# Attention strips by three transfers a unit, and second-half maxima joined with the first keys' maxima by one instruction

## The chip, the core and the metric

The kernel runs on one NeuronCore of a Trainium2 chip. The metric is the device time of one execution in microseconds. A core has five engines that take their own instructions in order: TensorE (PE in the profile; PEld is its weight loads), VectorE (DVE), ScalarE (ACT), GpSimd (POOL) and SyncE (SP), which here only issues transfers (DMAs). An engine waits for another by semaphores. Matrix products go into PSUM, which is used here in banks of 128 x 512 float32.

## What is computed

Four blocks follow each other on x of shape (4, 1024, 256), each added to its input after a layer norm: an attention with 16 heads, a gated recurrence (FFN), a delta-rule attention, and the FFN again. The change touches the first block only:

```python
c_kv = x @ W_dkv.T
q = (x @ W_dq.T @ W_uq.T).reshape(B, T, nh, hs)          # 16 heads of 16
q_lat = einsum('bqhd,hdl->bhql', q, k_eff)               # k_eff from W_dq, W_uq, W_uk
attn = einsum('bhql,bkl->bhqk', q_lat, c_kv) / sqrt(hs)
attn = softmax(where(causal, attn, -inf), axis=-1)
y = einsum('bhql,hld->bqhd', einsum('bhqk,bkl->bhql', attn, c_kv), v_eff)
```

The kernel brings the latent form down to 16 rows a head for queries and keys, and folds the two value projections into one matrix, `ve`.

## The kernel before

**Units and passes.** The attention works in 16 units: 4 batches times 4 groups of 4 heads. A unit's scores are computed twice. As "first" (`ps_s1`, queries in PSUM's partitions) they yield the maximum of each row; as "second" (`ps_s2`, keys in the partitions) they yield exp(score - maximum), the weights. `quad(i, s)` does step s of ten (`STEPS`, L54) for the second pass of unit i and the first pass of unit i + 1 side by side, so that stage i works on two units; stage -1 has only the first pass of unit 0. A step is a piece of keys times queries, 384 or 512 columns wide, for four heads. Each head has its own group of 32 rows of the PE array, so four matmuls with 32 rows run at once.

**Strips.** To hold float32 accuracy with products of rounded numbers, keys and queries are split into a high part and a remainder. A head's 32 rows of `q` hold 16 rows of high parts and 16 rows of remainders; `kh` (keys' high parts) and `kl` (their remainders) hold their 16 rows twice. The high and low parts of all heads stand in DRAM in `kall` and `qall`; `feature` (L272) computes 128 rows by 512 columns of them (PE, ACT cast, DVE subtraction) and SP writes them (L287). `heads(i, j)` (L313) fetches head j's strips of unit i by six transfers of 16 rows by 4 KB (L324), so 24 a unit, all on SP's queue. Three buffers each of `kh`, `kl` and `q` rotate over the units. Unit 0's strips are made without DRAM by `first_feature` (L296), with `wk0` and `wq0`, whose columns are in the strips' order, and `second_half` (L124), which is 1 in the rows of remainders.

**Maxima.** `finish` (L416) reduces a first-pass bank on DVE. Where a piece has masked keys, L424 adds the mask and takes the maximum, starting from a constant for queries 0 to 511, and from `m0` for queries 512 to 1023; `m0` is the maximum over keys 0 to 511, taken by L430 in steps 3 to 6. Each L424 is followed by a read of the accumulator. `greatest(i, half)` (L464) turns a half's maxima: a PE transpose (L468), an ACT cast (L470), a DVE subtraction (L471), a write to DRAM `md` (L473) and two reads into `gr` (L475), which the second pass subtracts by a matmul with `minus`. Half 0 of unit i + 1 is called after step 4 of stage i; half 1 of unit i after step 0 of stage i, when the DVE operations of that step, of unit i + 1, have been issued.

**Order of the work.** The order is written out by hand (L519 to L606). All engines receive their instructions in the order in which the Python calls are made. `places[s]` lists what follows step s: features, projections, norms, `heads` and `greatest`. In stage -1 the remaining features of batch 0, `heads(1, 0..3)`, the values and `load(2)` are spread over steps 3 to 9 (L569), with the `heads` after all eight features. `values` runs two steps behind, between the two halves of a step. After stage 1, `load_ffn` (L567) issues 13 transfers on SP. PSUM has seven banks for scores and small products, taken in turn (`pss`, L74).

Of the kernel before, what the change touches and what calls it, by code (L numbers as in the profile page):

```python
# [10 lines left out]
F32 = mybir.dt.float32  # L11
# [3 lines left out]
ALU = mybir.AluOpType  # L15
AX = mybir.AxisListType
PSUM = bass.MemoryType.PSUM

P = 128
B, T, C = 4, 1024, 256  # L20
# [7 lines left out]
NH, HS = 16, 16  # L28
# [10 lines left out]
def attention(k, w, x):  # L39
# [6 lines left out]
    nc, tc = k.nc, k.tc  # L46
    NT = T // P
# [20 lines left out]
    with ExitStack() as es:  # L68
# [52 lines left out]
        qq = [wp.tile([P, T], F32R, name=f"q{i}") for i in range(3)]  # L121
        gr = [wp.tile([P, T], F32R, name=f"gr{i}") for i in range(2)]
        minus = wp.tile([P, P], F32R, name="minus")
        second_half = wp.tile([P, 1], F32, name="second_half")  # L124
        wk0, wq0 = (wp.tile([P, P], F32, name=n) for n in ("wk0", "wq0"))

        def first_rows():
            nc.gpsimd.memset(minus.bitcast(F32), -1.0)
            nc.gpsimd.memset(mb, 0.0)
            nc.gpsimd.memset(second_half, 1.0)  # L130
            nc.gpsimd.affine_select(
                out=mb, in_=mb, compare_op=ALU.is_ge, fill=NEG, base=0, pattern=[[1, P]], channel_multiplier=-1,
            )
            for j in range(4):
                d = second_half[ds(32 * j, 32), :]
                nc.gpsimd.affine_select(
                    out=d, in_=d, compare_op=ALU.is_ge, fill=0.0, base=-HS, pattern=[[0, 1]],
                    channel_multiplier=1,
                )
            for g in gr:  # L140
                nc.vector.memset(g.bitcast(F32), 0.0)

        VS = HS + 1
        vb = [wp.tile([P, NT, NH * VS + 32 - VS], F32, name=f"vb{i}") for i in range(2)]
# [26 lines left out]
        nc.scalar.activation(wq, ps.rearrange("p k m -> p (k m)"), AF.Copy, scale=1.0 / math.sqrt(HS))  # L171
        for a in range(2):
            nc.scalar.activation(
                wq0.rearrange("p (j a r) -> p j a r", j=4, a=2)[:, :, a],
                ps[:, 0, 0:64].rearrange("p (j r) -> p j r", j=4), AF.Copy, scale=-1.0 / math.sqrt(HS),
            )
        ps = pss.tile([P, KVL], F32, tag="s", name="ps_p1")
# [4 lines left out]
        nc.tensor.matmul(ps, p1, wdq, start=True, stop=True)  # L182
        for a in range(2):
            nc.scalar.copy(
                wk0.rearrange("p (j a r) -> p j a r", j=4, a=2)[:, :, a],
                ps[:, 0:64].rearrange("p (j r) -> p j r", j=4),
            )
        nc.scalar.copy(wk, ps)
# [83 lines left out]
        def feature(b, mc, n, name, wt, src, aside=False):  # L272

            bt = batches[b]
            if mc == n == 0:
                setattr(bt, name, dr.tile([2, C, T], F32R, tag=name, name=name))
            ps = pss.tile([P, 512], F32, tag="s", name="ps_f")
            nc.tensor.matmul(
                ps, wt[:, ds(mc * P, P)], getattr(bt, src)[:, ds(n * 512, 512)], start=True, stop=True
            )  # L280
            if aside:
                hl = sm.tile([P, 4, 512], F32, tag="p", name="hp", bufs=3)[:, 0:2].bitcast(F32R)
            else:
                hl = sm.tile([P, 2, 512], F32R, tag="hl", name="hl", bufs=2)
            nc.scalar.copy(hl[:, 0], ps)
            nc.vector.tensor_tensor(hl[:, 1], ps, hl[:, 0].bitcast(F32), ALU.subtract)
            nc.sync.dma_start(  # L287
                out=getattr(bt, name).bitcast(F32)[:, ds(mc * P, P), ds(n * 512, 512)].rearrange("a c t -> c a t"),
                in_=hl.bitcast(F32),
            )  # L290
# [5 lines left out]
        def first_feature(n, name):  # L296

            u, bt = units[0], batches[0]
            cols = ds(512 * n, 512)
            ps = pss.tile([P, 512], F32, tag="s", name="ps_f")  # L300
            keys = name == "k"
            nc.tensor.matmul(ps, wk0 if keys else wq0, (bt.ckv if keys else bt.qd)[:, cols], start=True, stop=True)
            if keys:
                nc.scalar.copy(u.kh[:, cols], ps)
                nc.vector.tensor_tensor(u.kl[:, cols], ps, u.kh[:, cols].bitcast(F32), ALU.subtract)
            else:
                hi = sm.tile([P, 2, 512], F32R, tag="hl", name="hl", bufs=2)[:, 0]
                nc.scalar.copy(hi, ps)
                nc.vector.scalar_tensor_tensor(
                    u.q[:, cols], hi.bitcast(F32), second_half, ps, ALU.mult, ALU.subtract  # L310
                )

        def heads(i, j):  # L313

            if j == 0:
                name_buffers(i)
            u = units[i]
            bt = batches[u.b]
            rs = ds(64 * u.g + HS * j, HS)
            k_, q_ = bt.kall.bitcast(F32), bt.qall.bitcast(F32)  # L320
            for a in range(2):
                to = ds(32 * j + HS * a, HS)
                for dst, src in ((u.kh, k_[0, rs]), (u.kl, k_[1, rs]), (u.q, q_[a, rs])):
                    nc.sync.dma_start(out=dst.bitcast(F32)[to, :], in_=src)  # L324

        def normed(b, after=False):

# [38 lines left out]
        def quad(i, s):  # L366
# [49 lines left out]
            def finish(one, j):  # L416
                ps = bank(one, j)
                if not one:
                    nc.scalar.activation(p[:, j, :width], ps[:, :width], AF.Exp)  # L419
                    return  # L420
                for at, qt, c0, n, _, _ in pieces:
                    if c0 + n == (qt + 1) * P:
                        junk = sm.tile([P, 512], BF16, tag="junk", name="junk")
                        nc.vector.tensor_tensor_reduce(  # L424
                            out=junk[:, :n], in0=ps[:, ds(at, n)], in1=mask[:, 512 - n :], scale=1.0,
                            scalar=-3e38 if qt < 4 else first.m0[:, j, qt - 4 : qt - 3],
                            op0=ALU.add, op1=ALU.max, accum_out=first.m[:, qt // 4, j, qt % 4 : qt % 4 + 1],
                        )
                    else:
                        nc.vector.tensor_reduce(  # L430
                            first.m0[:, j, qt - 4 : qt - 3], ps[:, ds(at, n)], AX.X, ALU.max
                        )
# [31 lines left out]
        def greatest(i, half):  # L464

            u = units[i]
            ps = pss.tile([16, P], F32, tag="s", name="ps_m")
            nc.tensor.transpose(ps, u.m[:, half].rearrange("p j q -> p (j q)"), k.ident)  # L468
            mT = sm.tile([16, 2, P], F32R, tag="mT", name="mT")
            nc.scalar.copy(mT[:, 0], ps)  # L470
            nc.vector.tensor_tensor(mT[:, 1], ps, mT[:, 0].bitcast(F32), ALU.subtract)  # L471
            d = dr.tile([16, 2, P], F32R, tag="md", name="md")
            nc.sync.dma_start(out=d.bitcast(F32), in_=mT.bitcast(F32))  # L473
            for a in range(2):
                nc.sync.dma_start(  # L475
                    out=u.gr.bitcast(F32)[ds(a, 4, step=32), ds(half * 512, 512)].rearrange("j (q t) -> j q t", q=4),
                    in_=d.bitcast(F32)[:, a].rearrange("(j q) t -> j q t", j=4),
                )
# [41 lines left out]
        with tc.manual_schedule():  # L520
# [19 lines left out]
            for f in rest[:2]:  # L540
                f()
            del rest[:2]
            for mc in range(KC):
                for n in range(2):
                    for name, wt, of in (("kall", wk, "ckv"), ("qall", wq, "qd")):
                        rest.append(
                            lambda mc=mc, n=n, name=name, wt=wt, of=of: feature(
                                0, mc, n, name, wt, of, name == "qall" or n == 1
                            )
                        )  # L550
            rest += [lambda j=j: vals(0, j) for j in range(0, NT, 2)]
            rest[-2:-2] = [lambda j=j: heads(1, j) for j in range(4)]
            rest.append(lambda: load(2))
            late = []
            LONG = (0, 1, 3, 4, 6, 7, 8, 9)
            for i in range(-1, NU):
# [8 lines left out]
                    late += [lambda g=g: first_cells(g) for g in "fic"]  # L565
                places = [[] for _ in range(NS)]
                if i < 0:  # L567
                    places[0] += rest[:2]
                    places[1] += rest[2:4]  # L569
                    for a, f in enumerate(rest[4:]):  # L570
                        places[3 + a * (NS - 3) // len(rest[4:])].append(f)
                    rest = []
                else:
                    for work, left in ((rest, NG - 1 - i % NG), (late, NG - i % NG)):
                        share = -(-len(work) // left) if left > 0 else len(work)
                        for a, f in enumerate(work[:share]):
                            places[LONG[a * len(LONG) // share]].append(f)
                        del work[:share]
                if i + 1 < NU:
                    places[4].append(lambda i=i: greatest(i + 1, 0))  # L580
                if 0 <= i < NU - 2:

                    for j in range(4):
                        places[2 + j].append(lambda i=i, j=j: heads(i + 2, j))
                if i >= 0:
                    units[i].p = {}
                    places[0].insert(0, lambda i=i: greatest(i, 1))
# [1055 lines left out]
```

## Time and profile before

| | us |
|---|---|
| median of 3 runs (lowest to highest) | 1326.14 (1324.3 to 1327.25) |
| the profiled execution | 1326.79 |
| its span, first to last instruction | 1325.1 |
| PE busy in the span | 1247.8 |
| DVE busy | 840.2 |
| ACT busy | 697.5 |
| POOL busy | 423.3 |

The mean granted clock of PE is 0.982. A line of the profile gives an operation with its line in the kernel, what it writes and reads, its partitions and sizes, how often it ran, its busy time and mean, and the idle time of its engine just before it with what ended that. In a timeline a line has the start, the length, and in brackets the idle time before it. SPq is SP issuing a transfer, not the transfer itself.

### The profile page before, as it was taken

The page shows a single profiled execution, that of the slowest core. Times are in us where ns is not written, and L with a number is a line of the kernel's source. Part 1 is how long each engine was busy: PE and PEld are TensorE (multiplying, and loading weights), DVE is VectorE, ACT ScalarE, POOL GpSimd, SP SyncE. Part 2 cuts the span into 40 slices and gives each one's busy share as a digit, 9 for nine tenths or more (in the row PEclk, how much of TensorE's full clock was granted, in tenths as well). Part 3 has the DMA queues.
Part 4 walks back from the last instruction along what each step waited for, and adds up shares of the span by engine and source line. Part 5 has one row for each costly group of instructions (what it writes and reads, how often), then busy time and mean ns, then how long its engine had stood idle before and what let it go on. Part 6 is the DMA issues. An engine that isn't in the chain of part 4 may idle for free. (4 is left out here: it accounts for less than half of the span.)

```text
span 1325.1 us, 36572 instructions
## 1 busy us (share of the span) xinstructions
PE 1247.8 (94%) x14596; PEld 776.4 (59%) x14596; DVE 840.2 (63%) x2440; ACT 697.5 (53%) x1626; POOL 423.3 (32%) x681
## 2 busy tenths in 40 slices
PE   7899899999999999999999999898988999899997
PEld 3454455545555555555444766665655677677886
DVE  6786678787787877886122454468879767533333
ACT  3266566666666666666623456445655544334432
POOL 1040002323033110122100245346888745535220
PEclk9799899999999999999999999999999999999999
DMA  3812621334221422220300223215364532333210
GB/s 96 208 51 70 186 67 48 79 96 146 68 53 41 133 79 59 67 51 4 112 17 0 78 75 90 80 26 166 99 169 112 139 90 75 111 102 85 64 64 32
DMA packets 118649, 112.23 MB, mean 85 GB/s; under 512 B 46672, under 2 KB 103504, under 8 KB 118480
## 3 DMA queue, kind: packets, MB, share of 16 engines
q1 hardware_dynamic: 95200, 100.39, 27.6%
q10 hardware_dynamic: 23280, 9.51, 2.7%
q8 instruction: 115, 1.88, 0.6%
q14 instruction: 54, 0.44, 0.1%
HBM read 65.22 MB, written 44.63 MB: 83 GB/s over the span
## 5 line engine op out<-in xcount | busy, mean ns | idle before, releaser
L419 ACT ACTIVATE p<-ps_s 128x512 f32<-128x512 f32 (+1 forms) x640 | 319.3, 554 | 199.7 <-PE ps_s L410 196.5
L410 PE MATMUL ps_s<-kh,q 32*128 32x512 f32 (+3 forms) x768 | 189.3, 425 | 8.8 <-DMA q<-qall 5.1
L430 DVE TENSOR_REDUCE m<-ps_s 128x1 f32<-128x512 f32 x256 | 163.0, 681 | 34.9 <-PE ps_s L410 34.5
L410 PE MATMUL ps_s<-q,kh 32*128 32x512 f32 (+3 forms) x768 | 163.2, 424 | 0.4
L488 PE MATMUL ps_y<-p,vb 128*32 128x512 f32 (+3 forms) x1536 | 158.3, 500 | 1.1 <-ACT ys L494 1.0
L410 PE MATMUL ps_s<-kl,q 32*128 32x512 f32 (+3 forms) x768 | 151.7, 357 | 0.0
L424 DVE CUSTOM_DVE_ANT_0 junk<-ps_s,mask,m 128x512 bf16<-128x512 f32 (+3 forms) x256 | 126.4, 545 | 38.3 <-PE ps_s L410 37.6
L424 DVE CUSTOM_DVE_ANT_0 junk<-ps_s,mask 128x512 bf16<-128x512 f32 (+3 forms) x256 | 112.3, 486 | 48.9 <-PE ps_s L410 48.5
L410 PE MATMUL ps_s<-q,kl 32*128 32x512 f32 (+3 forms) x768 | 131.2, 359 | 0.0
L410 PEld LDWEIGHTS ps_s<-q,kh 32*128 32x128 f32 x768 | 73.9, 184 | 77.1 <-issue 45.8
L512 POOL TENSOR_TENSOR xa<-xa,yt 128x256 f32<-128x256 f32 x32 | 23.4, 731 | 275.7 <-DVE yt L508 275.7
L410 PEld LDWEIGHTS ps_s<-kh,q 32*128 32x128 f32 x768 | 89.1, 185 | 28.1 <-ACT p L419 9.8
L410 PE MATMUL ps_s<-gr,minus 32*128 32x512 f32 (+3 forms) x768 | 98.2, 365 | 6.1 <-DMA gr<-md 4.9
L391 PEld LDWEIGHTS <-identb 128*128 128x128 bf16 x512 | 34.4, 98 | 88.2 <-issue 85.8
L410 PEld LDWEIGHTS ps_s<-kl,q 32*128 32x128 f32 x768 | 81.4, 188 | 0.0
L205 POOL TENSOR_SCALAR rs<-mv 128x2 f32<-128x2 f32 x24 | 5.5, 230 | 236.6 <-DVE mv L204 236.6
L410 PEld LDWEIGHTS ps_s<-gr,minus 32*128 32x128 f32 x768 | 67.6, 187 | 19.7 <-DMA gr<-md 5.3
L1120 DVE SCALAR_TENSOR_TENSOR gate<-gate 128x256 f32<-128x256 f32 (+1 forms) x56 | 29.4, 524 | 76.3 <-ACT gate L1099 76.1
L1080 PE MATMUL ps_gate<-xnT,ffn_wi 128*128 128x256 f32 (+1 forms) x224 | 66.0, 418 | 3.5 <-DVE hh L1193 3.3
L1198 POOL TENSOR_TENSOR x<-x,hh 128x256 f32<-128x256 f32 x56 | 44.0, 800 | 75.0 <-ACT hh L1197 54.2
L772 PE MATMUL ps_kqv<-wa,h 128*128 128x512 f32 x128 | 65.5, 634 | 2.4 <-ACT h L762 2.3
L410 PEld LDWEIGHTS ps_s<-q,kl 32*128 32x128 f32 x768 | 67.2, 186 | 0.0
(228 smaller groups left out, 2626.5 us busy)
## 6 DMA issues: line engine op xcount, KB each, us to landing
x<-x SPq DMA_DIRECT2D x30, 512.0 KB
kh<-kall SPq DMA_DIRECT2D x120, 64.0 KB
kl<-kall SPq DMA_DIRECT2D x120, 64.0 KB
q<-qall SPq DMA_DIRECT2D x120, 64.0 KB
kall<-hl SPq DMA_DIRECT2D x14, 512.0 KB
qall<-hl SPq DMA_DIRECT2D x12, 512.0 KB
kept<-gs ACTq DMA_DIRECT2D x32, 192.0 KB
gl<-kept SPq DMA_DIRECT2D x32, 192.0 KB
```

Of the source, the lines that this page charges most:

```text
L205: nc.gpsimd.tensor_scalar(rs, mv[:, :, 1], EPS, None, ALU.add)
L391: nc.tensor.matmul(ps[:, ds(at, P)], identb, mb, start=x == 0 and (False, j) not in begun, stop=True, skip_group_check=True,)
L410: nc.tensor.matmul(ps[:, ds(at, n)], a, m, start=x == 0 and (one, j) not in begun, stop=last, skip_group_check=True,)
L419: nc.scalar.activation(p[:, j, :width], ps[:, :width], AF.Exp)
L424: nc.vector.tensor_tensor_reduce(out=junk[:, :n], in0=ps[:, ds(at, n)], in1=mask[:, 512 - n :], scale=1.0, scalar=-3e38 if qt < 4 else fir ...
L430: nc.vector.tensor_reduce(first.m0[:, j, qt - 4 : qt - 3], ps[:, ds(at, n)], AX.X, ALU.max)
L488: nc.tensor.matmul(u.y[ds(32 * j, 32), q0:], vb[u.b % 2][:, kt, ds((4 * u.g + j) * VS, 32)], u.p[s][:, j, ds(at, n)], start=kt == 0, stop= ...
L512: nc.gpsimd.tensor_tensor(xs, xs, yt.rearrange("p n j d -> p n (j d)"), ALU.add)
L772: nc.tensor.matmul(dst, hT(c, kc), wt[:, kc, :], start=kc == 0, stop=kc == KC - 1)
L1080: nc.tensor.matmul(ps, f["w" + "fic"[j]][:, kc, ds(m * P, P)], k.xnT[:, kc, t, ds(at, width)], start=kc == 0, stop=t == 0 and kc == KC - 1,)
L1120: nc.vector.scalar_tensor_tensor(acts[1], acts[1], 1.0, acts[2], ALU.add, ALU.mult)
L1198: nc.gpsimd.tensor_tensor(x[:, b, :], x[:, b, :], h, ALU.add)
```

## The change

Strips: `heads` now issues one transfer of 128 rows for each of `kh`, `kl` and `q`, called for x = 0, 1, 2 after steps 2, 3 and 4. For keys, 64 rows of DRAM are read with each row repeated; for queries the high part and the remainder of a row follow each other. So a head's 32 rows now alternate between the two parts. `wk0`, `wq0` and the column vector (now `odd`, summed from the identity by one DVE reduction instead of a memset and four selects on POOL) follow that order.

Stage -1: the features of the first 128 rows are placed after steps 2 and 3, the three `heads` of unit 1 at the head of the work after step 4, the other features after steps 4 to 7, the values after steps 7 to 9. All eight features use tiles of the pool of `p` (six did before).

Maxima: L424 starts from the constant in both halves, and `greatest(i, 1)` first joins `u.m[:, 1]` with `u.m0` by one DVE maximum of 128 x 16.

```diff
-                nc.gpsimd.affine_select(
-                    out=d, in_=d, compare_op=ALU.is_ge, fill=0.0, base=-HS, pattern=[[0, 1]],
...
+            nc.vector.tensor_reduce(odd, k.ident[:, ds(1, P // 2, step=2)], AX.X, ALU.add)
...
-                wq0.rearrange("p (j a r) -> p j a r", j=4, a=2)[:, :, a],
+                wq0.rearrange("p (j r a) -> p j r a", j=4, a=2)[:, :, :, a],
...
-            rs = ds(64 * u.g + HS * j, HS)
-            k_, q_ = bt.kall.bitcast(F32), bt.qall.bitcast(F32)
-            for a in range(2):
-                to = ds(32 * j + HS * a, HS)
-                for dst, src in ((u.kh, k_[0, rs]), (u.kl, k_[1, rs]), (u.q, q_[a, rs])):
-                    nc.sync.dma_start(out=dst.bitcast(F32)[to, :], in_=src)
+            rs = ds(64 * u.g, 64)
+            if x < 2:
+                dst, src = (u.kh, u.kl)[x], bt.kall.bitcast(F32)[x, rs].unsqueeze(1).broadcast_to([64, 2, T])
+            else:
+                dst, src = u.q, bt.qall.bitcast(F32)[:, rs].rearrange("a r t -> r a t")
+            nc.sync.dma_start(out=dst.bitcast(F32), in_=src)
...
-                            scalar=-3e38 if qt < 4 else first.m0[:, j, qt - 4 : qt - 3],
+                            scalar=-3e38,
...
             u = units[i]
+            if half:
+                nc.vector.tensor_tensor(u.m[:, 1], u.m[:, 1], u.m0, ALU.max)
             ps = pss.tile([16, P], F32, tag="s", name="ps_m")
...
-                            lambda mc=mc, n=n, name=name, wt=wt, of=of: feature(
-                                0, mc, n, name, wt, of, name == "qall" or n == 1
-                            )
+                    for y, (name, wt, of) in enumerate((("kall", wk, "ckv"), ("qall", wq, "qd"))):
+                        first[2 + n if mc == 0 else 4 + 2 * n + y].append(
+                            lambda mc=mc, n=n, name=name, wt=wt, of=of: feature(0, mc, n, name, wt, of, True)
...
-            rest[-2:-2] = [lambda j=j: heads(1, j) for j in range(4)]
-            rest.append(lambda: load(2))
+            for y in range(3):
+                first[4].insert(y, lambda y=y: heads(1, y))
+            for j in range(0, NT, 2):
+                first[NS - 3 + (j + 2) // 4].append(lambda j=j: vals(0, j))
+            first[NS - 1].append(lambda: load(2))
...
-                    for j in range(4):
-                        places[2 + j].append(lambda i=i, j=j: heads(i + 2, j))
+                    for y in range(3):
+                        places[2 + y].append(lambda i=i, y=y: heads(i + 2, y))
```

## The prediction

> **What bounds the kernel now.** I read the page's busy shares, then the table by 10 us stretches, then what PE waited for, and last the timeline of three places. The page's slices first (each is 33 us; the attention is the first 19):
>
> ```profile
> PE   7899899999999999999999999898988999899997
> ...
> DVE  6786678787787877886122454468879767533333
> ...
> PEclk9799899999999999999999999999999999999999
> ```
>
> PE is nine tenths busy, except in slices 1, 2 and 5. After the attention PE runs matmuls back to back to 752 us, so what the attention gains or loses should arrive at the end one to one. The weak places in the stretches (columns: length, PE, PEld, DVE, ACT, POOL busy, granted clock, DMA share, GB/s):
>
> ```profile
> 50.00:60.00 10.00, 7.01 (x27) 3.77 (x25) 4.03 (x20) 1.67 (x3) 0.00 (x0) 0.50 1.07 122
> 60.00:70.00 10.00, 7.88 (x68) 4.47 (x66) 6.53 (x29) 3.83 (x9) 3.89 (x6) 0.50 0.57 135
> ...
> 150.00:160.00 10.00, 5.41 (x30) 1.97 (x34) 2.65 (x5) 2.54 (x5) 0.72 (x1) 0.66 0.52 154
> ```
>
> At 50 to 70 us, step 0 of unit 0, PE waits at half clock for the strips of unit 1; SP issues the last of 24 at 58.26:
>
> ```profile
> 58.26 0.30 SPq L324 DMA_DIRECT2D q<-qall  x1
> ```
>
> ```profile
> 56.27 0.76 PE L410 MATMUL ps_s<-kh,q 32*128 32x512 f32 x1 [2.54 <-DMA q<-qall]
> ...
> 62.29 0.76 PE L410 MATMUL ps_s<-kh,q 32*128 32x512 f32 x1 [2.12 <-DMA q<-qall]
> ```
>
> At 149.67 PE stands 4.91 us for gr, queued on SP behind load_ffn. Everywhere else in the attention PE is full by the page. That is only partly true: it waits for banks inside its overlapped matmuls, as the next part shows.
>
> **1. The join (the largest term).** L468 transposes the maxima of a unit's second half at the end of step 0 of the next stage. Before, these maxima are finished one step earlier. After, the join stands ahead of the transpose on DVE, and the order of instructions in the changed kernel puts it behind all four mask-and-max operations of step 0, which belong to the next unit. The transpose gains a wait on DVE. PE and DVE at this place in unit 3, before:
>
> ```profile
> 185.97 0.28 PE L468 MATMUL ps_m<-ident,m 128*16 128x128 f32 x1
> 186.08 0.27 PE L391 MATMUL ps_s<-mb,identb 128*128 128x128 bf16 x2
> 186.29 0.43 PE L410 MATMUL ps_s<-q,kh 32*128 32x384 f32 x1
> 186.71 0.44 PE L410 MATMUL ps_s<-kh,q 32*128 32x384 f32 x1
> ...
> 187.83 0.86 PE L488 MATMUL ps_y<-p,vb 128*32 128x256 f32 x16
> ```
>
> ```profile
> 186.71 0.69 DVE L424 CUSTOM_DVE_ANT_0 junk<-ps_s,mask 128x512 bf16<-128x512 f32 x1
> 187.32 0.08 DVE L424 DVE_READ_ACCUMULATOR2_ANT m<- 128x1 f32 x1
> 187.32 0.27 DVE L471 TENSOR_TENSOR mT<-ps_m,mT 16x128 fp32r<-16x128 f32 x1
> ```
>
> PE reaches L468 at 185.97; DVE is through with the four at 187.32, 1.35 us later. The join has no row: bounded below by the 0.08 us of a read of the accumulator, above by the 0.27 of the mT subtraction; I take 0.20, from the delta stage's m<-m,mt 128x30 (0.204). PE starts 0.06 after a DVE end (hl ends at 315.61, the gr matmul behind it starts at 315.67). So PE stands 1.35 + 0.20 + 0.06 = **1.6 us**. Queued behind L468 are all later matmuls: features, then step 1. The distance is 1.3 to 1.4 in all of units 1 to 14; unit 15 has no next unit and no wait.
>
> What is given back: step 1 in unit 3 already waits for banks. From its first strip product (186.29) to its values (187.83) are 1.54 us; in units where a latent projection stands between, and DVE and ACT catch up meanwhile, the same work takes 0.72. After a stall of 1.6 the banks are free, so 0.82 comes back. By this measure: units 3, 4, 7, 8, 12, 13, 14 lose 0.8 each (5.6); unit 11 (1.32 there) loses 1.0 and unit 6 (1.07) loses 1.3; units 1, 5, 9, 10 have nothing to give back, 1.6 each (6.4). Sum **+14.3 us**; bounds 10 (0.7 each) and 22.4 (1.6 each). Unit 2 loses nothing: its 4.91 us for gr simply become shorter. mT, md and gr run 1.2 to 1.6 later, but so does PE, and gr is used three steps on.
>
> Does a stall of 1.6 us lower the clock? The nearest row says no:
>
> ```profile
> 1130.13 1.13 PE L1080 MATMUL ps_gate<-xnT,ffn_wi 128*128 128x256 f32 x4 [1.60 <-DVE hh L1193]
> ```
>
> The stretch 1125 to 1135 around it has a granted clock of 1.00; the gap of 4.91 gave 0.66.
>
> **2. Strips in three transfers, unit 1's issued earlier.** 24 issues of 64 KB become 3 of 512 KB; bytes stay the same. Before, SP spaced the issues some 0.5 us; from the first (45.26) to the last (58.26) are 13.0 us. Large transfers moved 276 to 343 GB/s (load_ffn, 140 to 148 us), so 1.5 MB needs some 5 us. In the changed order the three stand behind only four of the features' writes, not eight. The first four writes come from steps 2 and 3; the fourth was issued at 37.70 before, so I expect about 36, its landing near 38.5, the strips by 44. They are wanted at 52, so the wait goes. What is late next: nothing but the clock, which fell at 46.4 while PE was merely sparse, and stays 0.50 there for all I can see. Step 0 of unit 0 lasted 52.09 to 63.58, 11.5 us. Step 1, at the same clock and without a wait, lasted 3.2 for 384 columns with 0.7 of masks; for 512 that is 2.5 x 1.33 + 0.7 = 4.0. With the new join wait 5.7. Gain 5.8, and DVE (9.93 of 10 us busy in 40 to 50) reaches unit 0 some 0.5 earlier through part 3: **-6 us**. Bounds: -11 if the clock is full there (step 0 then 3 us, steps 1 and 2 a us shorter each), and +1 if the strips still come late. The features' eight buffers now rotate through three tiles; the eighth cast waits for the fifth write, about 45 us, when it is due anyway: nothing, or 2 us at worst.
>
> [...] Here the stretch 40 to 50 shows PE 9.50 of 10 us busy and a clock of 0.82. [...]
>
> **3. Constant start of the second half's maxima.** Two rows, equal shapes, with and without the start from m0:
>
> ```profile
> L424 DVE CUSTOM_DVE_ANT_0 junk<-ps_s,mask,m 128x512 bf16<-128x512 f32 x60 | 42.6, 747 | 14.7 <-PE ps_s L410 14.3
> ...
> L424 DVE CUSTOM_DVE_ANT_0 junk<-ps_s,mask 128x512 bf16<-128x512 f32 x56 | 36.4, 687 | 9.3 <-PE ps_s L410 9.0 <-issue 0.2
> ```
>
> 60 ns x 16 a unit = 1 us of DVE, less 0.2 for the join. Most lies beside PE: DVE waits for PE before half of these. PE's and its weight loads' waits put down to L424 are 7.6 us in all, most of it before unit 0. I take **-1.5**; bounds 0 and -7.6.
>
> **4. Unit 2's gr.** md is issued at 148.70, paced by load_ffn from 139.6, which doesn't move. The gap shrinks from 4.9 to 3.3 (that is the unit's free join wait), and the half clock of 6.8 us may be shorter: **-1**; bounds 0 and -4.
>
> Costed at nothing: SP's freed issue time (idle otherwise); the order of rows (the strided casts of wk0 and wq0 run before x's features need them); four selects fewer on POOL and one reduction more on DVE (both ahead of the first load's landing); two features' buffers from another tile.
>
> **The sum**, on the profiled execution (span 1325.1, 1326.79 with what lies around it, 0.65 above the median 1326.14): 1326.79 + 14.3 - 6 - 1.5 - 1 = **1332.6 us**.
>
> **Rivals.**
> *The start outweighs the join.* Place: unit 0. If PE is at full clock there, part 2 gives -11; with part 3 at -4, part 4 at -2 and the join at its lower bound of 10, the sum is -7: 1320. It decides from the point where parts 2 and 3 together pass 14 us. For it: the half clock is this kernel's own doing at 43 to 46 us. Against: the same sparse work stays there.
> *Nothing is given back.* If step 1's bank waits come from the latency of exp and maximum rather than from being late, they stay: 22.4 - 6 - 1 = +15.4: 1342. If the clock also fell at each stall, several us more. For it: ACT also has mT to cast, behind the stall. Against: the 0.72 in three units.
> *The three transfers are not faster.* If a transfer with a repeated row runs on a part of the engines only, 1.5 MB could take the old 12 us or more, and unit 0 waits as before: part 2 is 0 and the sum +11.8: 1338.6. For it: no row shows such a transfer. Against: rows of 4 KB as before, 64 of them outermost.
> [...]
>
> **Chances.** Forecast 0.58 (1328 to 1338; 0.08 of it within 0.2%); start outweighs 0.20 (0.15 faster, 0.05 within); nothing given back 0.13; transfers not faster 0.09. 0.2%, 2.7 us, is about what a measurement of this kernel tells from no change. Faster 0.15, same 0.13, slower 0.72. Range 1321 to 1342: it takes in the bounds of the join and most of the start.
>
> **What would show it.** Right: L468 of every second transpose idle about 1.6 us and released by the join; no wait for q at 52 to 63; L424 all near 687 ns at 512; step 0 of unit 0 near 6 us; the attention's end some 6 us later. Wrong: no PE gap at L468, or gaps of 1.6 with units as long as before (then PE's slack was larger than I measure), or a clock of 1.00 through 50 to 60.

## The result and the profile after

The changed kernel takes 1340.09 us (median of 4 runs, 1337.64 to 1340.77) beside 1326.7 (4 runs, 1324.3 to 1329.36): a ratio of 1.0096, 95% interval 1.0078 to 1.0115. The forecast was 1332.6. Slower was right, but the loss, 13.4 us, is more than twice the 5.8 of my sum. The profiled execution took 1340.77 us, its span is 1338.8, the mean granted clock 0.978 (0.982 before). In the quoted lines of the changed kernel the line numbers are its own: maximum with mask L418, join L462, transpose L464, strips L318.

The page's slices after the change (33 us each):

```profile
PE   7899899999999999999999989999888999999997
...
DVE  6876677677777777777132444467978767534333
...
PEclk9799899999989999999999999989999999999999
```

DVE is down a tenth here and there, and the row of the clock has something new: an 8 in the twelfth slice (368 to 402 us), in the middle of the attention, where before stood only nines. The table by stretches, at the places shown before (columns as there):

```profile
50.00:60.00 10.00, 7.80 (x73) 4.61 (x71) 8.14 (x39) 5.23 (x11) 1.13 (x3) 0.95 0.76 248
60.00:70.00 10.00, 9.89 (x101) 5.71 (x100) 6.89 (x29) 4.92 (x11) 5.62 (x6) 0.71 0.29 107
150.00:160.00 10.00, 9.61 (x73) 3.58 (x69) 5.30 (x10) 6.51 (x13) 0.00 (x0) 0.77 0.58 202
```

**The start did what was forecast.** 50 to 60 us holds 73 matmuls where it held 27. The strips of unit 1 are three issues on SP, from 37.57 us on, and the DMA view of 30 to 60 us (40 slices of 0.75 us) shows 366, 388 and 333 GB/s from 39.75 to 42 us, where the bytes are all theirs. The 407 behind 44 us counts the next feature's write too. The strips are in by 46 us, six before they are wanted:

```profile
37.57 0.63 SPq L318 DMA_DIRECT2D kh<-kall  x1
38.26 0.59 SPq L318 DMA_DIRECT2D kl<-kall  x1
38.95 0.55 SPq L318 DMA_DIRECT2D q<-qall  x1
```

```profile
GB/s 0 0 115 374 391 380 139 205 377 385 385 63 147 366 388 333 126 87 273 407 407 258 10 0 4 18 360 382 360 388 350 180 246 382 385 365 119 25 8 0
```

No wait for q is left. Unit 0's second transpose ends at 56.91 us, 6.9 earlier than before (63.79), its new stall included.

**The stall is there, with the length forecast.** Unit 3, PE and then DVE:

```profile
182.68 0.27 PE L464 MATMUL ps_m<-ident,m 128*16 128x128 f32 x1 [1.60 <-DVE m L462]
182.79 0.27 PE L385 MATMUL ps_s<-mb,identb 128*128 128x128 bf16 x2
```

```profile
181.76 0.69 DVE L418 CUSTOM_DVE_ANT_0 junk<-ps_s,mask 128x512 bf16<-128x512 f32 x1
182.37 0.08 DVE L418 DVE_READ_ACCUMULATOR2_ANT m<- 128x1 f32 x1
182.37 0.17 DVE L462 TENSOR_TENSOR m<-m,m 128x16 f32<-128x16 f32 x1
```

The join stands behind the four maxima of the next unit, and PE behind the join. What PE waited for in the attention, summed over it (us in all, times, longest):

```profile
PE ps_m L464 <- DVE m L462: 23.7, 15, 1.6
```

Fifteen times, units 0 to 14, 23.7 us.

**What I had not expected is what follows some of these stalls.** Unit 5's stall, in four stretches of 3.4 us:

```profile
246.60:250.20 3.60, 3.60 (x50) 2.12 (x45) 2.46 (x17) 2.27 (x6) 1.02 (x1) 1.00 0.02 5
250.20:253.60 3.40, 1.79 (x20) 0.66 (x20) 2.34 (x9) 2.05 (x4) 0.00 (x0) 0.99 0.00 0
253.60:257.00 3.40, 3.40 (x5) 1.22 (x5) 1.29 (x5) 0.25 (x1) 1.12 (x3) 0.50 0.02 5
257.00:260.40 3.40, 3.40 (x43) 1.90 (x42) 1.80 (x7) 2.73 (x6) 2.27 (x2) 1.00 0.46 159
```

PE is busy for 1.79 of 3.40 us in the stretch that holds the stall; for the next 3.4 us the clock is 0.50, and five matmuls fill the stretch. The profile's records of the granted clock show such a half-clock stretch (start, length) behind the stalls of units 0 (59.00, 6.83 us), 5 (253.56, 3.41), 7 (342.31, 3.41), 8 (379.85, 6.83), 12 (536.87, 3.41) and 14 (608.55, 3.41). Before the change there was none between 159 and 855 us.

At the end of the attention the changed kernel is 16.4 us behind (665.37 against 648.93); in the span it is 13.7. The 2.7 between say little: what follows the attention took 676.2 us before, 673.4 after and 670.2 to 675.3 in the kernels below, though nothing in it is changed.

### The profile page after: what moved, and what is told of

Same layout as the page of the kernel before. It is cut to its first block, busy times and chain, and to the rows that moved or that the text cites. A ratio compares the mean times of both kernels' runs of the same rounds, so it can differ in the third digit from the quotient of the medians.

```text
span 1338.8 us, 36102 instructions
## 1 busy us (share of the span) xinstructions
PE 1246.8 (93%) x14596; PEld 771.5 (58%) x14596; DVE 829.7 (62%) x2457; ACT 698.0 (52%) x1626; POOL 421.7 (31%) x676
## 5 line engine op out<-in xcount | busy, mean ns | idle before, releaser
L418 DVE CUSTOM_DVE_ANT_0 junk<-ps_s,mask 128x128 bf16<-128x128 f32 (+3 forms) x512 | 225.2, 487 | 98.8 <-PE ps_s L404 97.1
L424 DVE TENSOR_REDUCE m<-ps_s 128x1 f32<-128x512 f32 x256 | 163.0, 681 | 32.5 <-PE ps_s L404 32.1
L484 PE MATMUL ps_y<-p,vb 128*32 128x512 f32 (+3 forms) x1536 | 161.3, 509 | 1.1 <-ACT ys L490 1.0
L404 PE MATMUL ps_s<-q,kh 32*128 32x512 f32 (+3 forms) x768 | 160.1, 427 | 0.4
L404 PEld LDWEIGHTS ps_s<-kh,q 32*128 32x128 f32 x768 | 87.4, 188 | 23.5 <-ACT p L413 7.9
L404 PE MATMUL ps_s<-gr,minus 32*128 32x512 f32 (+3 forms) x768 | 92.1, 361 | 3.9 <-DMA gr<-md 2.9
L404 PEld LDWEIGHTS ps_s<-gr,minus 32*128 32x128 f32 x768 | 61.6, 187 | 16.7 <-DVE m L418 3.5
L1076 PE MATMUL ps_gate<-xnT,ffn_wc 128*128 128x256 f32 (+1 forms) x224 | 65.9, 417 | 1.1 <-ACT gate L1095 0.6
```

Of the source, the lines that this page charges most:

```text
L404: nc.tensor.matmul(ps[:, ds(at, n)], a, m, start=x == 0 and (one, j) not in begun, stop=last, skip_group_check=True,)
L418: nc.vector.tensor_tensor_reduce(out=junk[:, :n], in0=ps[:, ds(at, n)], in1=mask[:, 512 - n :], scale=1.0, scalar=-3e38, op0=ALU.add, op1= ...
L424: nc.vector.tensor_reduce(first.m0[:, j, qt - 4 : qt - 3], ps[:, ds(at, n)], AX.X, ALU.max)
L484: nc.tensor.matmul(u.y[ds(32 * j, 32), q0:], vb[u.b % 2][:, kt, ds((4 * u.g + j) * VS, 32)], u.p[s][:, j, ds(at, n)], start=kt == 0, stop= ...
L1076: nc.tensor.matmul(ps, f["w" + "fic"[j]][:, kc, ds(m * P, P)], k.xnT[:, kc, t, ds(at, width)], start=kc == 0, stop=t == 0 and kc == KC - 1,)
```

## The experiments

My theory after the comparison: the join costs its stall, carried on as the prediction has it, and on top of that half the clock for 3.41 or 6.83 us behind those stalls that leave PE busy for too small a part of a window (1.79 of 3.40 us, 0.53, in unit 5). By a window I mean one of the stretches of 3.413 us whose borders are those of the half-clock stretches in the records: the starts above lie whole multiples of 3.413 us from each other. The rival: the low clock and the gaps only take the place of other waits, and the loss lies in DVE's or the banks' new order, or in the strips. Each kernel was timed in five rounds beside the kernel before: the first four beside 1326.82 us (17 runs), the others beside 1326.14 (17 runs).

**1. The join one step earlier**

```diff
         def greatest(i, half):
...
-            if half:
-                nc.vector.tensor_tensor(u.m[:, 1], u.m[:, 1], u.m0, ALU.max)
...
+                    places[NS - 1].insert(0, lambda i=i: join(i + 1))
```

> The changed kernel, with the join issued one step earlier: behind the last maximum of step 9, ahead of step 0 of the next stage. The transpose stays where it was. DVE then has the join done before PE reaches the transpose, as it had the maxima before the change.
> Theory 1 (the join's stall of 1.6 us in 14 units, and the half clock that follows some of them, are the whole loss): the gaps at the transpose go, and with them the windows of half clock between 250 and 650 us; what stays is the gain of the strips (7 to 8), of unit 2's gr (2) and of the shorter maxima (1.5): 1314 to 1318 us, faster than both kernels.
> Theory 2 (the loss lies in the new order of the strips or in later banks, and the gaps at the transpose merely take the place of other waits): the gaps go but other waits come, 1330 us or more.

Measured: **1314.64 us**, ratio 0.9903 (0.9881 to 0.9925). The join is done ahead of the next step's maxima, and PE goes through the transpose without a gap. DVE and then PE in unit 3 of this kernel (its lines: join L460, transpose L466):

```profile
173.09 0.17 DVE L460 TENSOR_TENSOR m<-m,m 128x16 f32<-128x16 f32 x1
173.68 0.69 DVE L418 CUSTOM_DVE_ANT_0 junk<-ps_s,mask 128x512 bf16<-128x512 f32 x1 [0.41 <-PE ps_s L404]
```

```profile
175.12 0.39 PE L404 MATMUL ps_s<-q,kl 32*128 32x512 f32 x1
175.46 0.28 PE L466 MATMUL ps_m<-ident,m 128*16 128x128 f32 x1
175.57 0.27 PE L385 MATMUL ps_s<-mb,identb 128*128 128x128 bf16 x2
```

The clock is not lowered between 149 and 752 us. Theory 1 holds; no other wait comes in. The same 16 joins, moved by one step, are worth 25 us.

**2. A filler in the stall**

```diff
-            ps = pss.tile([16, P], F32, tag="s", name="ps_m")
+            whole = pss.tile([P, 512], F32, tag="s", name="ps_m")
+            ps = whole[:16, 0:P]
+            if half and i + 1 < NU:
+                for _ in range(1):
+                    nc.tensor.matmul(whole[:, ds(P, 384)], k.ident, mask[:, 0:384], start=True, stop=True)
```

> The changed kernel, with one additional matmul of 128 x 128 x 384 that nobody reads (into unused columns of the transpose's bank), ahead of the second half's transpose in units 0 to 14. It needs some 0.4 us (256 columns take 0.27) and lies in the stall: PE stands 1.2 us in place of 1.6, while the transpose waits for the join as late as before.
> Theory 1a (the clock is lowered where PE is busy for only about 0.53 of a window of 3.41 us; with the filler it is 0.65): no half clock behind any of the stalls. The changed kernel's profile has six such windows between 250 and 650 us, each worth up to 1.7 us: 1340.1 less some 8 to 10 is 1330 to 1332 us.
> Theory 1b (the clock falls for another reason, such as the row-tiled work that follows, or the drops cost nothing): the drops stay or go, and the time is that of the changed kernel, 1339 to 1341 us.

Measured: **1331.42 us**, ratio 1.0032 (1.0018 to 1.0046). The filler took 0.91 us, not 0.4: the profile counts it as two matmuls (x2 below, and 14626 matmuls in all beside 14596, 30 more for 15 fillers), so the 0.27 that I took for one of 256 columns was for half of one. Unit 5 again, four stretches around the same place, and the transpose:

```profile
245.50:248.90 3.40, 3.40 (x46) 2.07 (x38) 2.27 (x15) 2.07 (x6) 0.85 (x1) 1.00 0.02 5
248.90:252.30 3.40, 2.73 (x23) 1.02 (x23) 2.38 (x9) 2.09 (x4) 0.00 (x0) 1.00 0.00 0
252.30:255.70 3.40, 3.40 (x35) 1.63 (x34) 2.14 (x8) 1.46 (x4) 1.25 (x3) 1.00 0.02 5
255.70:259.10 3.40, 3.40 (x38) 1.89 (x38) 1.24 (x6) 2.19 (x5) 2.14 (x2) 1.00 0.60 195
```

```profile
250.57 0.91 PE L467 MATMUL ps_m<-mask,ident 128*128 128x384 f32 x2
252.15 0.28 PE L468 MATMUL ps_m<-ident,m 128*16 128x128 f32 x1 [0.67 <-DVE m L462]
```

The transpose comes as late after the products as in the changed kernel, but the clock stays at 1.00 behind all fifteen stalls. Work that nobody needs, put into a wait, saves 8.7 us (1340.09 to 1331.42): theory 1a. It also separates stall from clock: this kernel has the stalls without the clock's part.

**3. The strips alone (maxima as before)**

```diff
-                            scalar=-3e38,
+                            scalar=-3e38 if qt < 4 else first.m0[:, j, qt - 4 : qt - 3],
...
-            if half:
-                nc.vector.tensor_tensor(u.m[:, 1], u.m[:, 1], u.m0, ALU.max)
```

> The changed kernel with the maxima as before: the second half starts from the first keys' maxima, and there is no join. Only the strips and the order of stage -1 are changed.
> Theory 1: the whole gain without the loss: 6.8 plus the 1.4 us of unit 0's stall are 8, and 1 to 2 for unit 2's gr: 1316 to 1318 us.
> Theory 2 (the strips or their order cost later units time): 1322 us or more.
> Against the kernel with the early join it gives the price of the constant start: 1.5 us slower than that one if my term for it holds, nothing if DVE's time lies beside PE's anyway.

Measured: **1316.24 us**, ratio 0.9927 (0.9902 to 0.9952). The strips and their order are pure gain; theory 2 is out. Against the kernel with the early join the two intervals overlap. Stage by stage the traces do separate them: from unit 0's second transpose to the end of the attention the early join is 2.7 us shorter, 0.2 to 0.45 in each of seven stages, 0.1 or less in the others. The groups of DVE show where it is from: here the start from m0 costs 126.7 us for 256 operations, the constant start 112.4.

```profile
L418 DVE CUSTOM_DVE_ANT_0 junk<-ps_s,mask,m 128x512 bf16<-128x512 f32 (+3 forms) x256 | 126.7, 547 | 40.3 <-PE ps_s L404 39.5
...
L418 DVE CUSTOM_DVE_ANT_0 junk<-ps_s,mask 128x512 bf16<-128x512 f32 (+3 forms) x256 | 112.4, 487 | 38.1 <-PE ps_s L404 37.6
```

**4. The maxima alone (strips as before)**: the join and the constant start, put into the kernel before.

> The kernel before with the change of the maxima alone (constant start, join ahead of the transpose); strips and stage -1 as before.
> Theory 1: the loss without the gain. Changed kernel less before is +13.4; without the gain of 7 to 8 of the strips +21: 1346 to 1350 us, with gaps of 1.6 us at the transposes and half clock behind about half of those that lie inside one window of 3.41 us.
> Theory 2: less than 1340 us, because the strips have a part in the loss.

Measured: **1345.76 us**, ratio 1.0148 (1.012 to 1.0176), a quarter of a us below the expected range. PE waits 23.5 us in all for the join, as in the changed kernel, and the clock is at half behind the stalls of units 3, 5, 8, 12 and 14 (0.979 in the mean). So the loss belongs to the maxima. In the times the two parts do not quite add: -10.6 and +18.9 give +8.3, and 13.4 were measured; the three intervals, some 2.5 to 3.7 us each way, leave room for that. At the end of the attention they nearly do, -7.7 and +22.1 against +16.4; the rest is in the part behind it, which is the longest (676.2 us) in the one profile of before.

**5. A shorter filler**: as 2, with 128 columns.

> The changed kernel with a filler a third as long: one unread matmul of 128 x 128 x 128 ahead of the second half's transpose (the one of 384 columns took 0.93 us, so about 0.3). The gap becomes 1.3 us in place of 1.6; a window of 3.41 us that holds all of it is busy for 0.62.
> Theory 1a (a threshold near 0.53 to 0.58 of a window): no half clock behind these stalls, and 1330 to 1333 us, as with the longer filler.
> Theory 1b (any stall of over a microsecond lowers the clock if it falls well in a window): the half clock stays behind some five stalls, 1337 to 1341 us.

Measured: **1332.22 us**, ratio 1.0047 (1.003 to 1.0063). The gap is 1.04 to 1.10 us in units 1 to 14. A stretch that holds the whole of one (unit 8):

```profile
370.20:373.60 3.40, 2.30 (x31) 1.40 (x27) 2.02 (x9) 1.70 (x4) 0.00 (x0) 1.00 0.00 0
```

2.30 of 3.40 us busy, and no half clock behind any stall of units 1 to 14. Behind the full stalls the clock fell at shares from 0.50 to 0.53 in the changed kernel, and at 0.53 behind unit 12 of experiment 4 (1.80 of 3.40 us); at these 0.68 it did not: theory 1a. The profile is of the fastest of the eight runs (1326.62 us, clock 0.991; the others had 0.984 to 0.990), so for the others the median speaks alone: it lies in the range of 1a and 4.8 us below that of 1b.

**6 and 7. The two halves of the strips' part.** First the new order of stage -1 with the 24 transfers (and strips, maxima as before), then the three transfers in the old order:

```diff
+            for j in range(4):
+                first[4].insert(j, lambda j=j: heads(1, j))
```

> The kernel before with the new order of stage -1 alone: the transfers of unit 1's strips stand behind four features, but are still 24 of 64 KB; strips in the old order of rows, maxima as before.
> Theory 1 (the size of the transfers decides: SP needs some 0.5 us for each of the 24, 12 us, and the order only shifts when they begin): issued from about 37.5 to 49.5, landed by about 52, just when unit 0 wants them: most of the gain of the strips, 1317 to 1321 us.
> Theory 2 (the number of transfers is what holds them back, whatever their start): PE still waits in unit 0's step 0, and the time is nearer to the kernel before, 1322 to 1327 us.

```diff
+            rest[-2:-2] = [lambda y=y: heads(1, y) for y in range(3)]
```

> Three transfers a unit and the new order of rows, with the old order of stage -1 (the strips of unit 1 behind all eight features); maxima as before.
> Theory 1: the three are issued from about 45 to 47 in place of 45 to 58, 1.5 MB at some 385 GB/s land 4 to 5 us later, by 52: unit 0 hardly waits, 1316 to 1320 us, close to the kernel with strips and order changed (1316.2).
> Theory 2 (the early place gives the gain): 1323 to 1327 us.

Measured: **1319.55 us** (ratio 0.9955, 0.9939 to 0.9971) and **1319.45 us** (0.9949, 0.9928 to 0.997). Each alone brings nearly 7 us, both together 10.6. In each a wait is left, of 6.31 and 4.71 us, at different places. The first line is of the order alone, the second of the transfers alone:

```profile
54.83 2.07 PE L267 MATMUL ps_v<-ve,ckv 128*128 128x256 f32 x4 [6.31 <-ACT vb L268]
```

```profile
55.17 0.76 PE L404 MATMUL ps_s<-kh,q 32*128 32x512 f32 x1 [4.71 <-DMA q<-qall]
```

With 24 transfers SP issues them from 37.76 to 48.79 us, and it is now the remaining features' writes behind them that are late (the first at 49.27), so ACT, busy for 0.59 us between 40 and 50 us, stands for a tile that this write has to free, and PE behind ACT for the 6.31 us. With three transfers in the old place they start at 45.36, are issued by 48.4, and q is there at 55. My expectation for the second, landed by 52, was 3 us too early. Neither theory 2 holds.

**8. The FFN's loads earlier, with the early join**

```diff
+                if i == 1:
+                    places[5].append(k.load_ffn)
...
-                if i == 1:
-                    k.load_ffn()
```

> The kernel with the early join (1314.6 us), with one call moved: the FFN's 13 loads are issued behind step 5 of stage 1 in place of the end of that stage, so that nothing long stands on SP's queue when unit 2's md and gr are issued.
> Theory 1 (the wait for gr in unit 2, 4.9 us before, 2.9 in the changed kernel, is SP's queue behind these loads): no wait there, no half clock at 142 us (6.8 us at half speed, worth 3.4): 1308 to 1311 us.
> Theory 2 (the way through DRAM is that long anyway): a wait of 2 us or more stays at that place, 1313 to 1316 us.

Measured: **1309.48 us**, ratio 0.9873 (0.9852 to 0.9895), faster than both kernels and the lowest median here; its interval overlaps that of the early join, but its attention ends 3.7 us earlier (633.36 against 637.05). With the early join alone, unit 2 still had this wait (first fence, PE; then that kernel's SP), and with the loads moved it has none, and gr is issued 1.45 us behind md in place of 3.1:

```profile
143.98 0.80 PE L404 MATMUL ps_s<-gr,minus 32*128 32x512 f32 x4 [3.95 <-DMA gr<-md]
```

```profile
138.27 0.34 SPq L471 DMA_DIRECT2D md<-mT  x1
141.37 1.09 SPq L473 DMA_DIRECT2D gr<-md  x2
```

```profile
134.86 0.33 SPq L471 DMA_DIRECT2D md<-mT  x1
136.31 1.09 SPq L473 DMA_DIRECT2D gr<-md  x2
```

## Why the prediction was wrong in size

The profiles of before, of the changed kernel, of experiment 1 (no stall) and of experiment 2 (stall, no half clock) split the loss at the end of the attention. Each row but the first is counted from unit 0's second transpose:

| part | forecast, us | measured, us | from |
|---|---|---|---|
| up to unit 0's second transpose | -6 | -6.9 | 63.79 to 56.91 |
| the stalls, as carried on | +14.3 | +15.3 | experiment 2 less experiment 1 |
| the half clock behind them | 0 | +12.4 | after less experiment 2 |
| shorter maxima, unit 2's gr | -2.5 | -4.3 | experiment 1 less before |
| sum | +5.8 | +16.4 | |

**The step that failed** is the question "Does a stall of 1.6 us lower the clock? The nearest row says no." It does, behind six of fifteen. Of the 12.4 us, 10.7 lie in the six stages behind these stalls and 0.8 in unit 2, whose half clock behind the wait for gr was 3.41 us shorter with the filler; the rest is spread. In stages with a half-clock stretch of 3.41 us the changed kernel is 1.0 to 1.7 us longer than with the filler, in those with 6.83 us up to 2.7. These 12.4 us are from single profiles; by the medians fillers save 7.9 and 8.7, since the profile of experiment 2 happened to start 2.5 us later and took 1.4 us more behind the attention. Either is more than the whole miss of 7.5.

Why the row misled: the stretch from 1128.4 to 1131.9 around it, in the kernel before, is busy for 1.90 of 3.50 us, which is 0.54 and close to the shares at which the clock fell in the changed kernel. Stalls of the same length in the changed kernel went both ways: with 0.53 of a window busy the clock fell behind units 5, 7, 8, 12 and 14, and did not behind units 1 and 9 (nor, with 0.54, behind units 2 and 10). Behind unit 0 it fell with 0.50. One row with a yes or no so close to them was taken for a rule, and I had priced the opposite case at "several us more" in a rival with a chance of 0.13. The other gap that I named, 4.91 us with 0.66, should have led me to ask where between 1.6 and 4.9 the change lies, and to put the clock's price into the range.

The other steps, in order:

- *The stall's length and place*: right. 1.6 us forecast, 1.55 to 1.61 in units 1 to 14; the join took 0.17 (0.20 forecast).
- *What is given back*: right as to the units, with one exception, and too large in four of them. Experiment 2 less 1 shows give-backs of 0.84, 0.57, 0.82, 0.36, 0.84, 0.60 and 0.50 us after units 3, 4, 7, 8, 12, 13 and 14, where I had 0.8 each; 0.74 after unit 11 (0.6); at most 0.1 after units 1, 5, 9 and 10 (none). Unit 6 gave back nothing where I had 0.3. Unit 2's stall was free.
- *The strips*: right in size by the trace (6.9 against 6), and in part by luck. The half clock of 46 to 70 us, which I had kept, shrank to two stretches of 6.83 us (38.52 and 59.00), and step 0 lost its waits. So step 0 ran at full clock, where I had 0.50, and took 4.6 us (52.33 to 56.91) where I had 5.7; but it began 0.2 us later than before, where I had 0.5 earlier. The order of stage -1 and the transfers share the gain.
- *The constant start*: right in sign, small. DVE has the us a unit less that I worked out (14.3 in all), and 2.7 of them reach PE (experiment 1 less 3), where I took 1.5.
- *Unit 2's gr*: the gap went to 2.86 us, 3.3 forecast, but the clock fell there all the same. That FFN loads stand in front of md on SP was right (experiment 8).
- *One to one to the end*: 16.4 became 13.7, within what that part varies anyway.

**The rivals.** "Nothing is given back" has its time, 1342, close to the result and its reason refuted by the give-backs above; that the range, drawn out for it, holds the result is luck. "The transfers are not faster" is out: 333 to 388 GB/s. "The start outweighs the join" had its condition, full clock in unit 0, for step 0 alone, and parts 2 and 3 together stayed below the 14 us that it needed: 6.9 and 2.7.

The records of the clock in the changed kernel's profile explain a part of the unequal effects of equal stalls. The half-clock stretches up to the end of the attention start at 38.52, 59.00, 147.75, 253.56, 342.31, 379.85, 536.87 and 608.55 us, and their distances from the first are 6.0, 32.0, 63.0, 89.0, 100.0, 146.0 and 167.0 times 3.413 us. On this raster the stalls of units 3, 4, 6, 11 and 13 lay across a window's border, left PE busy for at least 0.59 of every window, and no half clock followed. It does not explain units 1, 2, 9 and 10, whose stalls lay inside one window. As to length, stalls of 1.4 to 1.6 us were enough in six cases of fifteen, and 1.04 to 1.10 us were not in units 1 to 14 of experiment 5.

What stays open: what it is that lowers the clock. PE's busy time does not order the cases with 0.53 and 0.54, and at 38.5 us the clock fell behind a window with 0.91 busy, where PE ran products of 32 rows with features between them, and at 147.75 us behind one with 0.63; in experiment 5 it fell behind unit 0's stall of 0.88 us too. I did not try to tell row-tiled products from whole ones by an experiment.

## What to carry to other kernels

An instruction that joins results of an earlier step belongs right behind that step: called where its result is needed, it queues behind whatever the same engine has been given meanwhile, and here 16 operations of 0.17 us cost 25 us. Price a new stall of PE twice, once as time carried on and once as half clock: here 3.41 or 6.83 us of it followed six of fifteen stalls of 1.4 to 1.6 us, where PE was busy for 0.50 to 0.53 of the 3.41 us before. Shortening the stalls of units 1 to 14 by a third, to 1.04 to 1.10 us, even with useless work, removed the second price here. When one row answers yes or no to a question of size, look how near it stands to the cases that answer otherwise.

## What the runs showed of the hardware that I had not expected

- Stalls of 1.4 to 1.6 us lowered the clock to a half for 3.41 or 6.83 us in six of fifteen cases, each time behind a window in which PE was busy for 0.50 to 0.53; stalls of 1.1 us (0.68 busy) or 0.67 us lowered it behind none of units 1 to 14, in one profile each of two kernels.
- All half-clock stretches of the changed kernel's attention lie on one raster of 3.413 us, and behind which of the equal stalls the clock fell differed between kernels (units 0, 5, 7, 8, 12, 14 after the change; 3, 5, 8, 12, 14 in experiment 4). Whether it also differs between executions of one kernel is not shown, as one of each was profiled.
- Three transfers of 512 KB, two of which read each row of 4 KB twice, moved 333 to 388 GB/s together, while SP needed 0.42 us of every 0.46 to issue 24 of 64 KB (experiment 6).
